# First part in two passes over an x kept on chip, v stored through GpSimd's queue, zeros of the banded weights written after the branch

## The chip, the cores and the metric

The kernel runs on one core of one Trainium2 chip. The metric is the device time of one execution in microseconds (us). All arithmetic is in float32.

## What is computed

The input x has shape 2 x 256 x 64 x 64. Two layers follow one another.

Layer 0 is attention over all 4096 positions of an image, with 8 heads of 32 channels, and a gated mix with the input:

```python
q = proj(Wq, bq) / math.sqrt(hd);  k = proj(Wk, bk);  v = proj(Wv, bv)
attn = softmax(einsum('bnd,bmd->bnm', q, k), axis=-1)
fuse = einsum('bnm,bmd->bnd', attn, v)
hybrid = conv1x1(concatenate([x, fuse], axis=1), Wf, bf)
x = hybrid * m + x * (1.0 - m)          # m: mask, resized to 64 x 64
```

Layer 1 is a channel gate, attention inside windows of 8 x 8 positions with 4 heads, a residual, a channel shuffle, two grouped 7 x 7 convolutions with batch norms, and a sigmoid gate:

```python
x = x * sigmoid(relu(xp @ ca_w1 + ca_b1) @ ca_w2 + ca_b2)
x = x + window_attention(x) @ out_w + out_b
y = relu(bn1(conv7x7(x, sa_w1)))
y = bn2(conv7x7(y, sa_w2))
return x * sigmoid(y)
```

## The kernel before

Positions are cut into 8 chunks of 512 per image, so there are 16 chunks in all. The program has three stretches.

**The first part** runs once over the 16 chunks. It loads a chunk of x (512 KB), multiplies it by Wq, Wk and Wv, and stores q, k and v in DRAM (tensors `qs`, `ks`, `vs`). Each result of two PSUM banks comes from `psum2`, of which there are three buffers. DVE copies q and k with their biases to SBUF (`qst`, `kst`, line 230), ACT squares the same PSUM values (`qsq`, `ksq`, line 231), and both take turns on a bank. TensorE sums the squares per head and token with `headsum` (`nrm`, line 254), and DVE keeps the largest (`nm`, line 265). ACT copies v (`vst`, line 258). The staging tiles have two buffers each, so that a copy waits for the store of two chunks ago. After the last chunk a bound on the scores comes out of `nm`: `top`, a small product `toprow`, `qk2`, `prod` and `flag`. Each engine loads `flag` and branches to one of two arms. Arm "a" uses no shift in the softmax, and it is the one that runs here.

All stores and x loads of the first part are issued by SP, whose DMA queue is q1 in the profile. Weights are loaded through ACT's queue (q10). GpSimd (POOL) issues the set-up of the convolutions through its own queue (q0): mask rows, batch-norm rows, small weights, and the zeros of `ws` (line 389), the DRAM tensor of banded weights, in 16 writes of 896 KB from a tile `zero` in SBUF. The set-up has DVE and ACT steps too (batch norms, products `m1` at line 335 and `m2` at line 374). In this stretch a scheduler of the framework orders each engine's queue.

**The slots** follow after the branch, in an order written out by hand. There are 1024, one for each image, chunk, half of the heads (g) and block of 128 keys (m). In a slot TensorE forms scores for four heads (`sa`, line 580), ACT takes exponentials (`ea`, line 590), TensorE multiplies by v (`ava`, line 609) and DVE adds up denominators (`suma`, line 611). The loop emits the scores of slot i + 2 ahead of the products of slot i. k and v come in pieces of four slots, 256 KB each, from a pool of three buffers: `load_piece` issues k and v of a piece two pieces ahead on SP. Exponentials have 8 buffers. The stage of a finished chunk (the rest of layer 0, and layer 1 up to the convolutions) is spread over later slots. Every sixth slot takes one step of the generator `bands`, which issues a GpSimd DMA that writes one diagonal band into `ws`:

```python
        load_q(0, 0)
        for n in range(AHEAD):
            load_piece(n)
        load_x(0, 0)
        for i in range(2):
            scores(i)()
        for i, (b, c, g, m) in enumerate(slots):
            ...
            if i % 6 == 1:
                next(banded, None)
```

The position of a step in this loop fixes its place in GpSimd's queue. It is no time: GpSimd goes on to its next instruction as soon as that instruction's own waits allow.

**The convolutions** begin among the last 64 slots, read `ws` and the padded rows `xs`, and end the program.

SBUF is reused between the stretches. The tiles of the first part are released ahead of the slots, and the first writers of tiles that lie over them wait for their last readers.

Of the kernel before, what the change touches and what calls it, by code (L numbers as in the profile page):

```python
# [54 lines left out]
def conv_seq_kernel(ctx: ExitStack, tc: tile.TileContext, a, out):  # L55
# [14 lines left out]
    def psum2(name):  # L70
        return ps["pair"].tile([P, 2, CH], F32, tag="s", name=name)

    def psum1(name):
        return ps["one"].tile([P, CH], F32, tag="h", name=name)
# [108 lines left out]

    nm = const.tile([P, B * NCHUNK], F32, name="nm")
    flag = const.tile([1, 1], I32, name="flag")
    with (
        tc.tile_pool(name="w0", bufs=1) as w0,
        tc.tile_pool(name="x0", bufs=3) as x0,
        tc.tile_pool(name="st0", bufs=2) as st0,
    ):  # L190
        def weight(n):
            return load(n, [P, KC, C], a[n].rearrange("(k p) o -> p k o", p=P), nc.scalar, w0)

        wq, wk, wv = weight("WqT"), weight("WkT"), weight("WvT")
        bias = {}
        for n in ("bq", "bk"):
            t = w0.tile([P, KC], F32, name=n)
            for g in range(KC):
                for j in range(HG):
                    h = HG * g + j  # L200
                    nc.scalar.dma_start(
                        t[32 * j : 32 * j + 32, g : g + 1], a[n][h % 2, :, h // 2 : h // 2 + 1]
                    )
            bias[n] = t

        for b in range(B):
            src = a["x"][b].rearrange("(k p) h w -> p k (h w)", p=P)
            for c in range(NCHUNK):
                x = x0.tile([P, KC, CH], F32, tag="x", name=f"x0_{b}_{c}")
                nc.sync.dma_start(x, src[:, :, c * CH : (c + 1) * CH])  # L210
                sqs = []
                for n, w in (("q", wq), ("k", wk)):
                    s = psum2(f"{n}0_{b}_{c}")
                    for g in range(KC):
                        for kc in range(KC):
                            rhs = x[:, kc, :]
                            if n == "q":
                                rhs = rhs.rearrange("p (r w c) -> p w r c", r=WS, w=NW)
                            nc.tensor.matmul(  # L219
                                s[:, g, :],  # L220
                                w[:, kc, g * P : (g + 1) * P],
                                rhs,
                                start=(kc == 0),
                                stop=(kc == KC - 1),
                            )
                    t = st0.tile([P, KC, CH], F32, tag=n, name=f"{n}st_{b}_{c}")
                    sq = st0.tile([P, KC, CH], F32, tag="sq", name=f"{n}sq_{b}_{c}", bufs=4)
                    bt = bias["b" + n]
                    for g in range(KC):
                        nc.vector.tensor_scalar_add(t[:, g, :], s[:, g, :], bt[:, g : g + 1])  # L230
                        nc.scalar.activation(  # L231
                            sq[:, g, :], s[:, g, :], AF.Square, bias=bt[:, g : g + 1]
                        )
                    sqs += [sq[:, g, :] for g in range(KC)]
                    if n == "q":
                        nc.sync.dma_start(q_s[b, c], t.rearrange("p g n -> p (g n)"))
                    else:
                        for g in range(KC):
                            nc.sync.dma_start(k_s[b, g, c], t[:, g, :])
                s = psum2(f"v0_{b}_{c}")  # L240
                sv = s.rearrange("p a (t o) -> p (a t) o", t=2)
                for m in range(4):
                    for kc in range(KC):
                        nc.tensor.matmul(
                            sv[:, m, :],
                            x[:, kc, m * P : (m + 1) * P],
                            wv[:, kc, :],
                            start=(kc == 0),
                            stop=(kc == KC - 1),
                        )  # L250

                norms = psum1(f"nrm_{b}_{c}")
                for i, sq in enumerate(sqs):
                    nc.tensor.matmul(
                        norms[32 * i : 32 * i + 32, :], headsum, sq, start=True, stop=True
                    )
                v = st0.tile([P, KC, 4, P], F32, tag="v", name=f"vst_{b}_{c}")
                nc.scalar.copy(
                    v.rearrange("p g m d -> p m g d"),
                    sv.rearrange("p m (g d) -> p m g d", g=KC),  # L260
                )
                for g in range(KC):
                    nc.sync.dma_start(v_s[b, g, c], v[:, g].rearrange("p m d -> p (m d)"))
                i = b * NCHUNK + c
                nc.vector.tensor_reduce(nm[:, i : i + 1], norms, AX.X, ALU.max)


        top = w0.tile([P, 1], F32, name="top")
        nc.vector.tensor_reduce(top, nm, AX.X, ALU.max)
        row = psum2("toprow")  # L270
        nc.tensor.matmul(row[0:1, 0, 0:P], top, ident, start=True, stop=True)
        qk2 = w0.tile([1, 2], F32, name="qk2")
        nc.vector.tensor_reduce(
            qk2, row[0:1, 0, 0:P].rearrange("p (i r) -> p i r", i=2), AX.X, ALU.max
        )
        prod = w0.tile([1, 1], F32, name="prod")
        nc.vector.tensor_mul(prod, qk2[:, 0:1], qk2[:, 1:2])
        nc.vector.tensor_scalar(flag, prod, (SAFE / SCALE0) ** 2, None, ALU.is_le)

    wf = load("WfT", [P, 2 * KC, C], a["WfT"].rearrange("(k p) o -> p k o", p=P), nc.scalar)  # L280
    bv = load("bv", [P, KC], a["bv"], nc.scalar)
# [103 lines left out]

    zero = cwp.tile([P, 2 * 32 * UW], F32, name="zero")
    nc.gpsimd.memset(zero, 0.0)
    for u in range(NU):
        nc.gpsimd.dma_start(w_s[u], zero)

    r1_s = dram.tile([rows, NU, UW], F32, name="r1s")
    nc.gpsimd.dma_start(
# [22 lines left out]
    def bands():  # L415
        band1 = w_s.rearrange("u p (m f) -> u (p m) f", f=UW)
        band2 = w_s.rearrange("u p (m f) -> u (p m) f", f=UW // 4)
        for q in range(4):
            for dy in range(KS):
                r0, r1 = max(0, dy - PAD), min(RB, RB + dy - PAD)  # L420
                p0, m0, n = 32 * q + 1 + r0, 1 + r0 - dy + PAD, r1 - r0
                k = KS * q + dy
                at0, step = p0 * 64 + m0, 64 + 1
                nc.gpsimd.dma_start(
                    band1[:, at0 : at0 + step * (n - 1) + 1 : step, :], spread(r1_s[k : k + 1], n)
                )
                yield
                for i in range(4):
                    at0, step = p0 * 256 + 128 + i * 32 + m0, 256 + 1
                    nc.gpsimd.dma_start(  # L430
                        band2[:, at0 : at0 + step * (n - 1) + 1 : step, :],
                        spread(r2_s[k : k + 1, :, i], n),
                    )
                    yield
            for i in range(4):
                at0 = 32 * q * 256 + 128 + i * 32 + 1
                nc.gpsimd.dma_start(
                    band2[:, at0 : at0 + RB, :], spread(r2_s[32 + q : 33 + q, :, i], RB)
                )
                yield  # L440
# [30 lines left out]
    def pipeline(arm, shifted, pools):  # L471
# [40 lines left out]
        def load_q(b, c):  # L512
            q = qp.tile([P, KC, CH], F32, tag="q", name=f"q{arm}_{b}_{c}")
            nc.sync.dma_start(q, q_s[b, c].rearrange("p (g n) -> p g n", g=KC))
            qts[b, c] = q
# [572 lines left out]
                stages.popleft()  # L1088

        banded = bands()  # L1090
        load_q(0, 0)
        for n in range(AHEAD):
            load_piece(n)
# [3 lines left out]
        for i, (b, c, g, m) in enumerate(slots):  # L1097
            now[0] = i
            if (b, c, g, m) == (B - 1, NCHUNK - 1, 0, 0):
                conv = convolve()  # L1100
                next(conv)
            if m % PB == 0:
                load_piece(i // PB + AHEAD)
            if g == KC - 1 and m == 0:
                nxt = (b, c + 1) if c + 1 < NCHUNK else (b + 1, 0)
                if nxt[0] < B:
                    load_q(*nxt)
            rest = scores(i + 2) if i + 2 < len(slots) else None
            products(i)
            if rest:  # L1110
                rest()
            if g == KC - 1 and m == NMB - 1:
                at(13, lambda b=b, c=c: stages.append(stage(b, c)))
            run_later()
            if i % 6 == 1:
                next(banded, None)
            if i % 4 == 0:
                run_stages()
# [98 lines left out]
```

## Time and profile before

| | |
|---|---|
| median of 3 runs | 3069.18 us (3069.12 to 3074.34) |
| profiled execution, own time | 3070.01 us |
| its span, first to last instruction | 3068.2 us |
| mean granted TensorE clock | 0.989 |
| first product of the first part begins | 5.29 us |
| first exponential of the slots begins | 222.47 us |
| zero writes of `ws` | 16 of 896 KB, median 17.1 us from issue to landing |
| bytes in the first 220 us | 53.23 MB, 242 GB/s |

In the profile a line gives the engine, the line of the kernel, the operation, the output and inputs by name, their shapes, and how many there are. A product in float32 appears as two records, so four products of q appear as "x8". In the timeline the first two columns are start and duration in us, and brackets at the end give the idle time before and what ended it. "SPq" and "POOLq" are DMAs issued by that engine.

### The profile page before, as it was taken

The numbers are of one execution on the slowest core, as the hardware profiler recorded it, in microseconds if no ns is written. First come the engines' busy times: TensorE is split into PE (matmuls) and PEld (weight loads), VectorE is DVE, ScalarE is ACT, GpSimd is POOL, SyncE is SP. The second block draws the span as 40 slices with busy tenths as digits, with TensorE's granted clock in tenths as the row PEclk, the third lists the DMA queues.
The fourth block names the chain that finished last, engine by engine and source line by source line (L and its number), as shares of the span: only waits on it lengthen the run. The fifth ranks groups of instructions, "written<-read, shape, count | busy, mean of one in ns | idle before, by whom it ended". The sixth has DMA issues, their size and how long they took to land.

```text
span 3068.2 us, 61291 instructions
## 1 busy us (share of the span) xinstructions
PE 2988.2 (97%) x25338; PEld 1015.0 (33%) x25338; DVE 2516.5 (82%) x1398; ACT 2450.6 (80%) x4122; POOL 344.7 (11%) x591
## 2 busy tenths in 40 slices
PE   8989989999999999999999999999999999999897
PEld 4442222232222222222232222323232223224675
DVE  3229989999999999998999999999999998988211
ACT  2239879898989898998989898989898988987423
POOL 7110000001010101010101001010101010000346
PEclk9989999999999999999999999999999999999998
DMA  6953112314141413242322214132413242314264
GB/s 197 356 162 76 59 50 64 67 63 72 59 81 60 75 64 69 66 75 68 66 66 61 66 59 73 59 74 61 78 60 68 70 71 66 109 57 134 61 203 97
DMA packets 160352, 264.20 MB, mean 86 GB/s; under 512 B 43944, under 2 KB 62620, under 8 KB 160064
## 3 DMA queue, kind: packets, MB, share of 16 engines
q1 hardware_dynamic: 133664, 221.72, 24.4%
q0 software_dynamic: 22432, 35.91, 8.4%
q8 instruction: 201, 3.29, 0.4%
q10 hardware_dynamic: 3968, 2.57, 0.3%
q14 instruction: 87, 0.71, 0.1%
HBM read 197.89 MB, written 65.21 MB: 86 GB/s over the span
## 4 chain that ended last, share of the span: by engine, by line
PE 70%; DVE 16%; issue 2%; DMA 2%; ACT 2%; POOL 1%; SPq 0%; DVEq 0%; ACTq 0%; POOLq 0%
PE sa L580 28%; PE ava L609 26%; DVE suma L611 15%; PE qka L748 4%; PE hya L677 4%; PE vwa L834 2%; PE c2a L1011 1%; POOL out_dram L1039 1%; PE c1a L987 1%; ACT ea L590 1%; PE opa L898 1%; DMA out_dram<-za 1%; PE sca L782 1%; PE rda L647 1%; PE pta L857 1%
## 5 line engine op out<-in xcount | busy, mean ns | idle before, releaser
L611 DVE TENSOR_TENSOR suma<-suma,ea 128x2048 f32<-128x2048 f32 x960 | 2198.7, 2290 | 86.0 <-ACT ea L590 1.8
L590 ACT ACTIVATE ea<-sa 128x512 f32<-128x512 f32 (+1 forms) x3072 | 2044.2, 745 | 85.0 <-PE sa L580 36.9
L580 PE MATMUL sa<-qa,ka 32*128 32x512 f32 x8192 | 1189.9, 641 | 8.2 <-DMA ka<-ks 8.0
L609 PE MATMUL ava<-ea,va 128*32 128x512 f32 x8192 | 1092.3, 605 | 0.3 <-ACT fa L619 0.3
L580 PEld LDWEIGHTS sa<-qa,ka 32*128 32x128 f32 x8192 | 333.1, 183 | 762.8 <-ACT ea L590 688.6
L609 PEld LDWEIGHTS ava<-ea,va 128*32 128x32 f32 x8192 | 161.6, 108 | 780.6 <-issue 754.3
L924 POOL DMA_DIRECT2D xs<-xo x94 | 65.9, 708 | 2353.5 <-DVE xo L909 2353.4
L1039 POOL DMA_DIRECT2D out_dram<-za x192 | 108.0, 571 | 128.1 <-DVE za L1033 92.4
L748 PE MATMUL qka<-ua,qkv_w 128*128 128x512 f32 x256 | 118.4, 605 | 0.7 <-DVE ua L738 0.7
L1033 DVE TENSOR_TENSOR za<-za,xla 128x768 f32<-128x768 f32 (+1 forms) x16 | 20.9, 1309 | 101.4 <-ACT za L1027 65.0
L1011 PE MATMUL c2a<-yca,wa 32*128 32x192 f32 (+1 forms) x1400 | 100.0, 427 | 0.3 <-ACT za L1021 0.3
L685 ACT ACTIVATE ta<-hya,bf 128x512 f32<-128x512 f32 x32 | 20.2, 684 | 96.9 <-PE hya L677 96.9
L1011 PEld LDWEIGHTS c2a<-yca,wa 32*128 32x128 f32 x1400 | 91.8, 316 | 10.9 <-issue 9.7
L689 DVE TENSOR_TENSOR ta<-ta,mca 128x512 f32<-128x512 f32 x32 | 22.0, 689 | 88.0 <-ACT ta L685 88.0
L1021 ACT ACTIVATE za<-c2a 128x384 f32<-128x384 f32 (+1 forms) x50 | 26.3, 578 | 79.7 <-DMA out_dram<-za 47.9
L803 ACT ACTIVATE ewa<-ewa,mxwa 128x64 f32<-128x64 f32 x256 | 85.5, 362 | 0.0
L611 DVE TENSOR_TENSOR suma<-ea,ea 128x2048 f32<-128x2048 f32 x32 | 73.1, 2286 | 15.0 <-DMA va<-vs 15.0
L231 ACT ACTIVATE qsq<-q,bq 128x512 f32<-128x512 f32 x32 | 22.0, 687 | 74.1 <-DVE qst L230 72.6
L430 POOL DMA_DIRECT2D ws<-r2s x112 | 69.5, 623 | 68.5 <-DMA xs<-xo 33.2
L761 ACT ACTIVATE qka<-qka,qkv_b 128x512 f32<-128x512 f32 x64 | 40.7, 694 | 44.2 <-PE qka L748 44.2
L987 PE MATMUL c1a<-xla,wa 128*32 128x192 f32 (+1 forms) x896 | 58.7, 413 | 14.2 <-DMA xla<-xs 14.2
L230 DVE TENSOR_SCALAR qst<-q,bq 128x512 f32<-128x512 f32 x32 | 24.0, 751 | 59.1 <-PE q L219 41.2
(139 smaller groups left out, 1674.7 us busy)
## 6 DMA issues: line engine op xcount, KB each, us to landing
ka<-ks SPq DMA_DIRECT2D x256, 256.0 KB
va<-vs SPq DMA_DIRECT2D x256, 256.0 KB
ws<-zero POOLq DMA_DIRECT2D x16, 896.0 KB, 17.1
wa<-ws SPq DMA_DIRECT2D x16, 896.0 KB
xs<-xo POOLq DMA_DIRECT2D x78, 140.0 KB, 7.2
xla<-xs SPq DMA_DIRECT2D x23, 420.0 KB
x<-in_x_dram SPq DMA_DIRECT2D x16, 512.0 KB
ks<-kst SPq DMA_DIRECT2D x32, 256.0 KB
```

The costliest lines, as they stand in the source:

```text
L430: nc.gpsimd.dma_start(band2[:, at0 : at0 + step * (n - 1) + 1 : step, :], spread(r2_s[k : k + 1, :, i], n),)
L580: nc.tensor.matmul(heads[j], k[r, cols], q[r, g, :], start=True, stop=not shifted)
L590: nc.scalar.activation(e[:, h, :], tile, AF.Exp, scale=SCALE0)
L609: nc.tensor.matmul(av[r, :], v[:, m % PB, r], e[:, j, :], start=start, stop=stop)
L611: nc.vector.tensor_add(total, first[0] if m == 1 else total, e)
L677: nc.tensor.matmul(s[:, oc, :], wf[:, kc, oc * P : (oc + 1) * P], xw[kc] if kc < KC else f[:, kc - KC, :], start=(kc == 0), stop=(kc == 2 ...
L748: nc.tensor.matmul(s[:, j, :], wqkv[:, kc, o : o + P], u[:, kc, :], start=(kc == 0), stop=(kc == KC - 1),)
L803: nc.scalar.activation(e[:, n, :], e[:, n, :], AF.Exp, bias=mx[:, n : n + 1], accum_out=rs[:, n : n + 1],)
L924: eng.dma_start(x_s[b, n, p + r0 : p + r1].rearrange("r g w -> g r w"), xo[64 * h : 64 * h + 64, oc, r0 - WS * c : r1 - WS * c, :],)
L987: nc.tensor.matmul(s[32 * j : 32 * j + 32, 0 : n * W], w[:, j, d, :], xs[k][:, 0:n, j, d : d + W], start=(d == 0), stop=(d == KS - 1),)
L1011: nc.tensor.matmul(tiles[j // 2][:, j % 2, 0 : n * W], w[r, d], y[r, 0:n, d : d + W], start=(d == 0), stop=(d == KS - 1),)
L1039: eng.dma_start(dst[b, i, r0:r1, UG * u : UG * u + UG, :], z[p + r0 : p + r1, :, nb * m + n, :],)
```

## The change

- The loop over chunks becomes two. Pass 1 loads x, forms q and k, and stores them. All 16 chunks of x stay in SBUF: the pool `x0` has one buffer per chunk, and is opened after the staging pool. Pass 2 forms v from them.
- The squares of q and k of a chunk go to one tile. DVE takes the largest of each four neighbouring tokens (`tops`, one instruction for 2048 elements), and `headsum` multiplies these 128 columns instead of 512 (function `norms`). It does so one chunk late, after the next chunk's q. The last chunk's norm and `flag` are computed during the first two chunks of pass 2.
- Stores of v are issued by GpSimd instead of SP.
- The 16 zero writes are replaced by one write of 896 KB to a DRAM tensor `zeros` in the first part, and four copies from there into `ws`, each for four of its 16 slices, as the first steps of `bands`. The source's first dimension has step zero. The rest of `bands` comes four steps later, and is drained ahead of the convolutions.
- One exponential of a single element (`warm`) stands ahead of the slots on ACT.

In the queues as built, GpSimd's four copies stand directly after its branch and ahead of all bands, each as 4 x 14 x 16384 floats, without a wait for another engine. The stores of v stand behind GpSimd's set-up. SP's order after the branch is q, k and v of pieces 0 and 1, x, mask, k and v of piece 2, as before. The first exponential and the load of x wait for the last stores of v.

```diff
-        tc.tile_pool(name="x0", bufs=3) as x0,
         tc.tile_pool(name="st0", bufs=2) as st0,
+        tc.tile_pool(name="x0", bufs=1) as x0,
...
+        def norms(i, tops):
+            s = psum1(f"nrm_{i}")
+            for n in range(2 * KC):
+                s_ = s[32 * n : 32 * n + 32, 0 : CH // 4]
+                nc.tensor.matmul(s_, headsum, tops[:, n, :], start=True, stop=True)
+            nc.vector.tensor_reduce(nm[:, i : i + 1], s[:, 0 : CH // 4], AX.X, ALU.max)
+
+        xs0, last = [], None
+        for i, (b, c) in enumerate(chunks):
+            x = x0.tile([P, KC, CH], F32, name=f"x0_{b}_{c}")
...
+                if n == "q":
+                    nc.sync.dma_start(q_s[b, c], t.rearrange("p g n -> p (g n)"))
+                    if i:
+                        norms(i - 1, last)
...
+            nc.vector.tensor_reduce(
+                tops, sq.rearrange("p g (n f) -> p g n f", f=4), AX.X, ALU.max
+            )
+            last = tops
...
+        for i, (b, c) in enumerate(chunks):
+            x = xs0[i]
+            s = psum2(f"v0_{b}_{c}")
...
             for g in range(KC):
-                nc.sync.dma_start(v_s[b, g, c], v[:, g].rearrange("p m d -> p (m d)"))
+                nc.gpsimd.dma_start(v_s[b, g, c], v[:, g].rearrange("p m d -> p (m d)"))
+            if i == 0:
+                norms(len(chunks) - 1, last)
+                nc.vector.tensor_reduce(top, nm, AX.X, ALU.max)
+            elif i == 1:
...
-    for u in range(NU):
-        nc.gpsimd.dma_start(w_s[u], zero)
+    zero_s = dram.tile([P, 2 * 32 * UW], F32, name="zeros")
+    nc.gpsimd.dma_start(zero_s, zero)
...
     def bands():
+        for u in range(0, NU, 4):
+            nc.gpsimd.dma_start(
+                w_s[u : u + 4].rearrange("u p f -> u (p f)"),
+                zero_s.rearrange("p f -> (p f)").unsqueeze(0).to_broadcast([4, P * 64 * UW]),
+            )
+            yield
...
         banded = bands()
+        nc.scalar.activation(warm, ones[0:1, 0:1], AF.Exp)
...
             if (b, c, g, m) == (B - 1, NCHUNK - 1, 0, 0):
+                for _ in banded:
+                    pass
```

More of the change, by code (lines that the diff above doesn't have):

```diff
@@ L185, in conv_seq_kernel @@
     flag = const.tile([1, 1], I32, name="flag")
+    warm = const.tile([1, 1], F32, name="warm")
     with (
         tc.tile_pool(name="w0", bufs=1) as w0,
-        tc.tile_pool(name="x0", bufs=3) as x0,
         tc.tile_pool(name="st0", bufs=2) as st0,
+        tc.tile_pool(name="x0", bufs=1) as x0,
     ):
@@ L204, in conv_seq_kernel @@
             bias[n] = t
-        for b in range(B):
-            src = a["x"][b].rearrange("(k p) h w -> p k (h w)", p=P)
[L208 to L242, printed above, removed]
@@ new lines, in conv_seq_kernel @@
+        chunks = [(b, c) for b in range(B) for c in range(NCHUNK)]
+        def norms(i, tops):
[7 more added lines that the diff above has]
+            x = x0.tile([P, KC, CH], F32, name=f"x0_{b}_{c}")
+            src = a["x"][b].rearrange("(k p) h w -> p k (h w)", p=P)
+            nc.sync.dma_start(x, src[:, :, c * CH : (c + 1) * CH])
+            xs0.append(x)
+            sq = st0.tile([P, 2 * KC, CH], F32, tag="sq", name=f"sq_{b}_{c}")
+            tops = st0.tile([P, 2 * KC, CH // 4], F32, tag="top4", name=f"top4_{b}_{c}")
+            for n, w in (("q", wq), ("k", wk)):
+                s = psum2(f"{n}0_{b}_{c}")
+                for g in range(KC):
@@ L243, in conv_seq_kernel @@
                     for kc in range(KC):
+                        rhs = x[:, kc, :]
+                        if n == "q":
+                            rhs = rhs.rearrange("p (r w c) -> p w r c", r=WS, w=NW)
                         nc.tensor.matmul(
-                            sv[:, m, :],
-                            x[:, kc, m * P : (m + 1) * P],
-                            wv[:, kc, :],
+                            s[:, g, :],
+                            w[:, kc, g * P : (g + 1) * P],
+                            rhs,
@@ L250, in conv_seq_kernel @@
                         )
[L252 to L255, printed above, removed]
-                    )
[L257 to L260, printed above, removed]
-                )
@@ L262, in conv_seq_kernel @@
-                for g in range(KC):
-                    nc.sync.dma_start(v_s[b, g, c], v[:, g].rearrange("p m d -> p (m d)"))
[L264 to L278, printed above, removed]
+                t = st0.tile([P, KC, CH], F32, tag=n, name=f"{n}st_{b}_{c}")
+                bt = bias["b" + n]
+                for g in range(KC):
+                    nc.vector.tensor_scalar_add(t[:, g, :], s[:, g, :], bt[:, g : g + 1])
+                    nc.scalar.activation(
+                        sq[:, g + KC * (n == "k"), :], s[:, g, :], AF.Square, bias=bt[:, g : g + 1]
+                    )
@@ new lines, in conv_seq_kernel @@
+                if n == "q":
+                    nc.sync.dma_start(q_s[b, c], t.rearrange("p g n -> p (g n)"))
+                    if i:
+                        norms(i - 1, last)
+                else:
+                    for g in range(KC):
+                        nc.sync.dma_start(k_s[b, g, c], t[:, g, :])
+            nc.vector.tensor_reduce(
+                tops, sq.rearrange("p g (n f) -> p g n f", f=4), AX.X, ALU.max
+            )
+            last = tops
+        row = psum2("toprow")
@@ new lines, in conv_seq_kernel @@
+        top = w0.tile([P, 1], F32, name="top")
+        for i, (b, c) in enumerate(chunks):
+            x = xs0[i]
+            s = psum2(f"v0_{b}_{c}")
+            sv = s.rearrange("p a (t o) -> p (a t) o", t=2)
+            for m in range(4):
+                for kc in range(KC):
+                    nc.tensor.matmul(
+                        sv[:, m, :],
+                        x[:, kc, m * P : (m + 1) * P],
+                        wv[:, kc, :],
+                        start=(kc == 0),
+                        stop=(kc == KC - 1),
+                    )
+            v = st0.tile([P, KC, 4, P], F32, tag="v", name=f"vst_{b}_{c}")
+            nc.scalar.copy(
+                v.rearrange("p g m d -> p m g d"),
+                sv.rearrange("p m (g d) -> p m g d", g=KC),
+            )
+            for g in range(KC):
+                nc.gpsimd.dma_start(v_s[b, g, c], v[:, g].rearrange("p m d -> p (m d)"))
[3 more added lines that the diff above has]
+            elif i == 1:
+                nc.tensor.matmul(row[0:1, 0, 0:P], top, ident, start=True, stop=True)
+                qk2 = w0.tile([1, 2], F32, name="qk2")
+                nc.vector.tensor_reduce(
+                    qk2, row[0:1, 0, 0:P].rearrange("p (i r) -> p i r", i=2), AX.X, ALU.max
+                )
+                prod = w0.tile([1, 1], F32, name="prod")
+                nc.vector.tensor_mul(prod, qk2[:, 0:1], qk2[:, 1:2])
+                nc.vector.tensor_scalar(flag, prod, (SAFE / SCALE0) ** 2, None, ALU.is_le)
@@ L417, in bands @@
         band2 = w_s.rearrange("u p (m f) -> u (p m) f", f=UW // 4)
+        for u in range(0, NU, 4):
+            nc.gpsimd.dma_start(
+                w_s[u : u + 4].rearrange("u p f -> u (p f)"),
+                zero_s.rearrange("p f -> (p f)").unsqueeze(0).to_broadcast([4, P * 64 * UW]),
+            )
+            yield
         for q in range(4):
```

## The prediction

> **What bounds the kernel now.** I read the page's busy shares, its chain that ended last, and then the timeline up to the first exponential, which is where the change lies.
>
> ```profile
> PE 2988.2 (97%) x25338; PEld 1015.0 (33%) x25338; DVE 2516.5 (82%) x1398; ACT 2450.6 (80%) x4122; POOL 344.7 (11%) x591
> ...
> PE 70%; DVE 16%; issue 2%; DMA 2%; ACT 2%; POOL 1%; SPq 0%; DVEq 0%; ACTq 0%; POOLq 0%
> ```
>
> TensorE sets the time nearly everywhere, so a microsecond of TensorE work or of TensorE waiting is a microsecond of the span. In the first part, one steady chunk on TensorE and the end of that part read (start, duration, what, idle time before):
>
> ```profile
> 162.52 3.70 PE L219 MATMUL q<-x,WqT 128*128 128x512 f32 x8
> 166.06 3.60 PE L219 MATMUL k<-x,WkT 128*128 128x512 f32 x8
> 169.49 3.62 PE L244 MATMUL v<-WvT,x 128*128 128x256 f32 x16
> 173.04 0.62 PE L254 MATMUL nrm<-qsq,headsum 128*32 128x512 f32 x2
> ...
> 174.04 3.70 PE L219 MATMUL q<-x,WqT 128*128 128x512 f32 x8
> ...
> 210.05 1.05 PE L452 MATMUL bvf<-bv,WfT 128*128 128x1 f32 x8
> 219.07 3.79 PE L580 MATMUL sa<-qa,ka 32*128 32x512 f32 x14 [7.96 <-DMA ka<-ks]
> ```
>
> A chunk takes 11.51 us: q 3.54, k 3.43, v 3.55, norms 0.99. Sixteen would be 184.2; from 5.29 to 208.6 they take 203.3. The other 19.1 are waits: about 3 at the start, 8.4 in chunks 3 and 4 (DVE and ACT wait there for small weight loads on GpSimd's queue), 7.4 in chunks 8 and 9 (stores stuck beside the zero writes). After the last product:
>
> ```profile
> 211.39 0.14 DVE L278 TENSOR_SCALAR flag<-prod 1x1 int32<-1x1 f32 x1
> 212.59 0.32 SPq L514 DMA_DIRECT2D qa<-qs  x1
> ...
> 221.18 1.28 ACT L590 ACT_TABLE_LOAD   x1 [12.43 <-PE sa L580]
> 222.47 3.90 ACT L590 ACTIVATE ea<-sa 128x512 f32<-128x512 f32 x6
> ```
>
> Flag, branch, first k load and table load lie one after another: 13.9 us from 208.6 to the first exponential at 222.47.
>
> **What the Trainium skill says.** "DMA: Bandwidth & Descriptors", section Queues, rings and completion order: each DMA engine round-robins between its queues by whole packets, whatever their size. The trace agrees. While the zeros were written (100 to 110 us; packets, MB, share):
>
> ```profile
> q0 software_dynamic: 502, 3.20, 76.6%
> q1 hardware_dynamic: 506, 0.96, 24.9%
> ```
>
> One packet each, although q0's are 7 KB and q1's 2 to 4 KB. The same page, Rules for kernel authors: an outermost zero-step dimension of c copies confines a DMA to at most c engines; nothing in this trace shows it. Its Latency and other measured facts: a DRAM-to-DRAM copy ran at some 207 to 214 GB/s; the trace has no large one, but its plateau of 417 GB/s, each byte touching DRAM once, halves to 208. "ScalarE: Activation LUTs", What ACT_TABLE_LOAD costs, has 1283 ns; the trace has 1.28 us.
>
> **Part by part: the first part.** Pass 1 keeps q (3.54), k (3.43) and norms. Norms multiply 128 columns instead of 512: a quarter of 0.99 plus switching, 0.5 taken (0.25 to 0.8). So 7.4 us a chunk on TensorE. DVE gets one maximum over 2048 elements per chunk; the nearest row has 512 in 0.68:
>
> ```profile
> L794 DVE TENSOR_REDUCE mxwa<-ewa 128x8 f32<-128x512 f32 x32 | 21.8, 682 | 42.5 <-ACT ewa L790 42.5
> ```
>
> An add of 2048 takes 2.29 (L611), so 2.3 (4 if groups of four cost extra). The norm's maximum falls from 0.69 to about 0.28 (L273's row, 128 elements). DVE then has 4 x 0.75 + 2.3 + 0.28 = 5.6 per chunk. Its dependent loop (maximum, copy, norm maximum, copy, copy, square, copy, square) is 2.3 + 0.75 + 0.28 + 0.75 + 0.75 + 0.8 + 0.75 + 0.75 = 7.1: just under TensorE. Walking the built queues with these rows: copies of chunk 4 stand behind the m1 product, whose loads end at about 51.5 (50.96 before; GpSimd starts its mask stores 1.2 later), some 7 us of waiting; those of chunk 6 behind the m2 products until about 73. From there TensorE paces; pass 1 ends at about 135.6.
>
> Pass 2 is 16 x 3.45 = 55.2, with the last norm and the small top product 0.7: last v product at **191.5**. Its stores move to GpSimd's queue: 32 issues of about 0.55, behind set-up that ends near 95, so none is late. Each copy (1.0) waits for the stores of two chunks ago: 6.9 us minus copy and two issues leaves 4.6 for landing; I take 2.5 to 3.5, so it is hidden. Sixteen x loads move ahead on SP; one is needed each 7.4 us, hidden. Branch and first loads now go beneath pass 2, as the flag is ready near 149. What is late next: the first exponential's buffer lies over the v staging, and its wait includes the last v stores: 0.2 + 1.0 + 1.2 + 2.5, so about 197. `warm` takes its 1.28 inside that wait. **Gain 222.5 - 197 = 25.5 us** (18 to 30).
>
> **The zeros.** Leaving the first part they take away the 7.4 of chunks 8 and 9, counted above. One 896 KB write remains there, hidden. Among the slots, nothing makes GpSimd wait between the four copies: a slot is only a place in its queue, so all four issue (4 x 0.55) right after its branch, data from about 196. Each is built as 4 x 14 x 16384 floats, first source step zero: 4 engines, 14 packets of 64 KB on each; four DMAs fill 16 engines once. 14.7 MB at 208 to 214 GB/s: **70 us** (37 if engines keep the 26 GB/s each that 417/16 gives).
>
> Who waits: SP's q1. Its order after the branch is q, k0, v0, k1, v1, then x, mask, k2, v2. The x load waits for the last v stores (its tile lies over them), so x, mask, k2 and v2 join q1 as the zeros start: 16 + 8 + 8 + 8 packets of 2 KB per engine. At one q1 packet per 64 KB packet only 14 pass in 70 us. Pieces need this pace:
>
> ```profile
> 229.76 0.32 SPq L507 DMA_DIRECT2D ka<-ks  x1
> 234.83 0.32 SPq L509 DMA_DIRECT2D va<-vs  x1
> 238.02 0.32 SPq L507 DMA_DIRECT2D ka<-ks  x1
> 243.15 0.32 SPq L509 DMA_DIRECT2D va<-vs  x1
> ```
>
> A pair every 8.3 us, 16 packets per engine: a neighbour packet above about 0.5 us starves it. At 70/14 it is 5 us. Slots 0 to 7 run on pieces 0 and 1. Scores of slot 8 are due 16.4 us after the first exponential (228.5 + 5 x 2.07 against 222.47), at 213.5; k2 lands at 196 + 70 + 2.5 = 268.5. TensorE waits 55 us and restarts at a low clock (0.70 in 222 to 232 before): 2 more. The bands queue behind the zeros on GpSimd, but the weights are only loaded at 2655.8 before; free. Afterwards k and v are ahead again.
>
> **Sum.** 3068.2 - 25.5 + 57 = 3099.7; with the 1.8 around the span 3101.5, against 3070.0 for the profiled execution; the median shown is 0.8 lower: **3101**.
>
> **Rivals.** (1) *No starvation, faster*: descriptors of 64 KB are chopped, or engines share by bytes. With 4 KB packets q1 would get a third of some 300 GB/s, above the 62 it needs (512 KB per 8.3 us). Then 3069 - 25.5 = 3044. Against it: the equal counts above, and 16 KB instruction packets on the page (q8: 201 packets, 3.29 MB) left whole. It decides below 0.5 us a packet. (2) *Fast copies*: 37 us, k2 at 235.5, wait 22 + 2: 3068. (3) *All four DMAs on the same four engines*: 56 packets there, 141 us at 26 GB/s; v3 at about 340 instead of slot 12's 227, some 112 lost: 3156. (4) *The maximum costs 4 us*: the loop is 8.8, 16 x 1.4 = 22 more on any case; little speaks for it.
>
> **How the numbers follow.** This kernel's measurement tells 0.2% (6 us) from no change. Chances: starvation at 70 us 0.47, all on four engines 0.13, fast copies 0.12, none 0.24, slow maximum 0.04. Slower: 0.47 + 0.13 + 0.02 + 0.04 = 0.66; same 0.07 (most of the rest of fast copies); faster 0.27. The likeliest case's own range is 3080 to 3120 (50 to 85 us of copying). To hold 8 in 10 the range reaches down to rival 1 and leaves out rival 3: 3040 to 3130.
>
> **What would show it.** Right: v products end near 191, first exponential near 197; then a TensorE gap of some 50 us before slot 8's scores, ended by DMA ka<-ks, with equal packet counts of q0 and q1 and few of both. Wrong: slots at 2.07 us through the zeros, or k2 landing within 20 us of issue; pass 1 above 8 us a chunk with DVE never idle; v copies that wait for v stores.

## Result and the profile after

The changed kernel takes 3091.68 us (median of 4 runs, 3087.66 to 3095.37) against 3069.57 us for the kernel before: a ratio of 1.0065, with a 95% interval of 1.005 to 1.008. The change makes the kernel 0.65% slower. The profiled execution took 3095.37 us with a span of 3093.6 us (before: 3068.2).

From the page of the changed kernel come the busy shares, the chain that ended last, and the group of the scores (busy time, mean ns of one, then the idle time before it and its releasers):

```profile
PE 2973.6 (96%) x25338; PEld 1013.4 (33%) x25338; DVE 2544.0 (82%) x1414; ACT 2450.1 (79%) x4123; POOL 356.3 (12%) x612
...
PE 83%; DVE 7%; DMA 4%; ACT 2%; POOL 2%; another core or an unknown queue 1%; issue 1%; SPq 0%; DVEq 0%; ACTq 0%; POOLq 0%
...
L602 PE MATMUL sa<-qa,ka 32*128 32x512 f32 x8192 | 1187.6, 641 | 38.9 <-DMA ka<-ks 35.8
```

TensorE is busy for 14.6 us less than before, yet the span is 25.4 us longer, so the time is in waits. The last line names the wait: the scores stand idle for 35.8 us until a load of k has landed.

The timelines of the changed kernel show the new DVE maximum, and one steady chunk of pass 1 on TensorE:

```profile
22.91 2.27 DVE L254 TENSOR_REDUCE top<-sq 128x512 f32<-128x2048 f32 x1
...
102.84 3.60 PE L233 MATMUL q<-x,WqT 128*128 128x512 f32 x8
106.28 2.74 PE L233 MATMUL k<-x,WkT 128*128 128x512 f32 x6
108.94 0.43 PE L215 MATMUL nrm<-top,headsum 128*32 128x128 f32 x8
109.30 1.13 PE L233 MATMUL k<-x,WkT 128*128 128x512 f32 x2
110.26 3.17 PE L233 MATMUL q<-x,WqT 128*128 128x512 f32 x7
```

From one q to the next is 7.42 us. The norms stand inside it, between the products of k, and TensorE has no pause. So far the change does what it says. Then the slots begin, in the timeline of all engines:

```profile
199.41 2.73 POOL L435 DMA_DIRECT2D ws<-zeros  x4 [0.53 <-issue]
201.36 5.80 ACT L612 ACTIVATE ea<-sa 128x512 f32<-128x512 f32 x9 [2.33 <-issue]
...
203.32 1.56 SPq L529 DMA_DIRECT2D ka<-ks  x1
...
215.85 1.14 PE L602 MATMUL sa<-qa,ka 32*128 32x512 f32 x8
...
253.83 2.09 PE L602 MATMUL sa<-qa,ka 32*128 32x512 f32 x8 [35.85 <-DMA ka<-ks]
253.96 0.65 POOL L446 DMA_DIRECT2D ws<-r1s  x1 [51.83 <-DMA ws<-zeros]
```

The four zero copies leave back to back at 199.41, and the first exponential begins at 201.36, 21.1 us earlier than before. The k of piece 2 is issued 4 us after the copies and is due at about 218. It lands at 253.8, in the same moment as the last bytes of the copies. The DMA view from 210 to 230 us shows how the time went (packets, MB, share of the 16 engines):

```profile
q0 software_dynamic: 96, 6.29, 93.6%
q1 hardware_dynamic: 96, 0.20, 4.8%
```

The queues pass equal numbers of packets, 96 to 96, but a zero packet is 64 KB and a q1 packet 2 KB. A turn of both takes a DMA engine 3.3 us (20 us x 16 engines / 96), nearly all of it for the zero packet, and q1 gets 10 GB/s of 325. From 220 to 250 us TensorE does nothing and its granted clock is 0.50 to 0.56; the first scores after the wait take 2.09 us instead of 1.14.

**Where the 25.4 us of the profiled execution lie:**

| place | us |
|---|---|
| first exponential at 201.36, not 222.47 | -21.1 |
| wait ahead of slot 8 | +35.9 |
| restart at a low clock (first slots after it 3.88 and 2.56 us apart, not 2.07) | +2.3 |
| won back around chunk 0's stage, 340 to 420 us; not traced | -2.8 |
| one pause of 3.5 us at 2040 and the slow products after it, in this execution | +4.7 |
| drift over the other slots | -0.2 |
| last exponential to GpSimd's last store | +1.8 |
| GpSimd's last store to the end | +4.8 |

Such a pause ("issue" in the waits, 2 to 4 us) shows in several of the runs below too; its cause is open. It may be part of why this execution is the slowest of the four; the other three have no trace.

### The profile page after: what moved, and what is told of

It is laid out like the page before. It is cut to its first block, busy times and chain, and to the rows that moved or that the text cites. A ratio compares the mean times of both kernels' runs of the same rounds, so it can differ in the third digit from the quotient of the medians.

```text
span 3093.6 us, 61287 instructions
## 1 busy us (share of the span) xinstructions
PE 2973.6 (96%) x25338; PEld 1013.4 (33%) x25338; DVE 2544.0 (82%) x1414; ACT 2450.1 (79%) x4123; POOL 356.3 (12%) x612
## 4 chain that ended last, share of the span: by engine, by line
PE 83%; DVE 7%; DMA 4%; ACT 2%; POOL 2%; another core or an unknown queue 1%; issue 1%; SPq 0%; DVEq 0%; ACTq 0%; POOLq 0%
PE sa L602 33%; PE ava L631 30%; DVE suma L633 6%; PE qka L770 4%; PE hya L699 4%; PE vwa L856 2%; PE v L268 2%; PE opa L920 2%; DMA wa<-ws 1%; PE c2a L1033 1%; POOL out_dram L1061 1%; PE k L233 1%; PE q L233 1%; PE c1a L1009 1%
## 5 line engine op out<-in xcount | busy, mean ns | idle before, releaser
L602 PE MATMUL sa<-qa,ka 32*128 32x512 f32 x8192 | 1187.6, 641 | 38.9 <-DMA ka<-ks 35.8
L244 ACT ACTIVATE sq<-q,bq 128x512 f32<-128x512 f32 x32 | 22.0, 687 | 65.2 <-DVE qst L243 58.0
L770 PEld LDWEIGHTS qka<-ua,qkv_w 128*128 128x128 f32 x256 | 46.0, 189 | 72.4 <-issue 58.8
```

Of the source, the lines that this page charges most:

```text
L602: nc.tensor.matmul(heads[j], k[r, cols], q[r, g, :], start=True, stop=not shifted)
L770: nc.tensor.matmul(s[:, j, :], wqkv[:, kc, o : o + P], u[:, kc, :], start=(kc == 0), stop=(kc == KC - 1),)
```

## Experiments

The theory, called **turns** below: the stall is set by the packets of q1 that stand ahead of piece 2, and by how long one packet of the zeros takes. Its first rival, **bytes**: the copies take the DMA bandwidth, and whatever their packets are, the loads wait until they are through. Other rivals put the loss into the two passes, the load of x, or GpSimd's new stores. In the experiments the kernel before ran at 3073 to 3075 us, 4 to 5 us above the result's, so ratios are compared. The times expected for the runs up to xlate start from the result's 3091.7 and would lie some 4 us higher on the scale of these runs. All times in the two right columns, and starts of the first exponential, are those of the profiled executions.

| kernel | median us | ratio to before, 95% interval | wait for loads in the first slots, us | GpSimd's last store to the end, us |
|---|---|---|---|---|
| changed kernel | 3091.7 | 1.0065 (1.005 to 1.008) | 35.9 | 11.3 |
| z28 | 3095.0 | 1.0070 (1.0053 to 1.0087) | 34.0 | 10.8 |
| z14 | 3075.8 | 1.0012 (1.0002 to 1.0023) | 19.4 + 2.1 | 11.0 |
| z7 | 3063.6 | 0.9965 (0.9952 to 0.9978) | 6.2 | 11.8 |
| zfirst | 3057.7 | 0.9960 (0.9946 to 0.9974) | 0 | 11.3 |
| full | 3062.6 | 0.9968 (0.9958 to 0.9978) | 0 | 11.6 |
| bz64 | 3095.5 | 1.0073 (1.0056 to 1.009) | 22.3 + 8.4 | 5.2 |
| vsp | 3094.3 | 1.0065 (1.0048 to 1.0082) | 36.6 in pass 2 | 5.4 |
| xlate | 3080.3 | 1.0022 (1.0014 to 1.003) | 26.9 | 11.2 |
| vact | 3058.6 | 0.9949 (0.9934 to 0.9963) | 0 | 6.7 |
| z7x | 3056.1 | 0.9945 (0.9931 to 0.996) | 0 | 11.9 |
| best | 3055.2 | 0.9936 (0.9915 to 0.9957) | 0 | 6.8 |

The last column of the kernel before is 6.5 us.

### z28, z14, z7: the same bytes in smaller packets

```diff
             nc.gpsimd.dma_start(
-                w_s[u : u + 4].rearrange("u p f -> u (p f)"),
-                zero_s.rearrange("p f -> (p f)").unsqueeze(0).to_broadcast([4, P * 64 * UW]),
+                w_s[u : u + 4].rearrange("u p f -> u (p f)").rearrange("u (n f) -> n u f", n=128),
+                zero_s.rearrange("p f -> (p f)")
+                .rearrange("(n f) -> n f", n=128)
+                .unsqueeze(1)
+                .to_broadcast([128, 4, P * 64 * UW // 128]),
             )
```

128 pieces give packets of 7 KB (z7); 64 give 14 KB (z14), 32 give 28 KB (z28).

> The changed kernel with its zero copies in packets of 28 KB instead of 64 KB; same bytes, same place. Turns (each DMA engine passes one packet of the zeros for one packet of q1): the changed kernel's trace shows 3.3 us per 64 KB packet, 19.7 GB/s per engine, so 1.4 us per 28 KB packet; k2 is the 32nd q1 packet of an engine after the x load is issued at 201.4, 32 x 1.5 = 48 us, past the end of the copies at about 246, so k2 lands as late as before, or a few us earlier: wait of TensorE ahead of slot 8 some 33 us, time 3088. Bytes (the loads wait because the copies take the bandwidth, whatever the packets are): 36 us, 3091.

> The changed kernel with its zero copies in packets of 14 KB. Turns: 0.7 us per packet of the zeros plus 0.1 for q1's own, k2 passes after 32 x 0.8 = 26 us, about 228; with some 2.5 us to land, TensorE waits about 15 to 20 us ahead of slot 8 (due 218), and v2 follows 6 us later: time about 3072 to 3076. Bytes: a wait of 36 us again, 3091.

> The changed kernel with its zero copies in packets of 7 KB, the size that the kernel before used for its zero writes. Turns: 0.36 us per packet of the zeros plus 0.1, k2 passes after 32 x 0.46 = 15 us at 216, v2 after 18 us: no wait ahead of slot 8, or up to 3 us; time 3091.7 - 36 = 3055 to 3058, faster than before. Bytes: 36 us, 3091.

The waits ahead of slot 8 were 34.0, 19.4 and 6.2 us for 28, 14 and 7 KB, against 35.9 for 64 KB (z14 waits another 2.1 us ahead of slot 12). From the TensorE timelines of z28, z14 and z7:

```profile
252.76 2.09 PE L605 MATMUL sa<-qa,ka 32*128 32x512 f32 x8 [34.02 <-DMA ka<-ks]
```

```profile
237.05 2.09 PE L605 MATMUL sa<-qa,ka 32*128 32x512 f32 x8 [19.39 <-DMA ka<-ks]
```

```profile
225.87 2.09 PE L605 MATMUL sa<-qa,ka 32*128 32x512 f32 x8 [6.17 <-DMA ka<-ks]
```

The same DMA view, 210 to 230 us, first z28, then z14, then z7:

```profile
q0 software_dynamic: 251, 6.28, 88.4%
q1 hardware_dynamic: 251, 0.48, 10.9%
```

```profile
q0 software_dynamic: 437, 5.82, 79.8%
q1 hardware_dynamic: 436, 0.82, 18.1%
```

```profile
q0 software_dynamic: 775, 5.38, 76.3%
q1 hardware_dynamic: 771, 1.43, 23.9%
```

The counts stay one to one, and q0 loses little (6.29 to 5.38 MB in 20 us), but q1 gets 2.6, 4.5 and 8 times as many packets. Bytes expected 36 us in all three; it falls. For 28 KB the k of piece 2 again lands with the last bytes of the copies (252.8), so almost nothing is gained, as turns expected. The edit also changes the order of the copies (the outermost dimension is 32, 64 or 128 instead of 4). z28 has the new order with packets that are still large, and waits nearly as long: the order is not what helps.

Two times missed. z28 took 3095.0, not 3088: about 4 us are the scale of these runs, and its profiled execution has three pauses of the kind named above (4.8 us). z7 took 3063.6, not 3055 to 3058, where turns expected at most 3 us of wait and got 6.2. The count was low: from 203 to 226 us q1 passed 691 packets, 43 per engine, and in z14 685 until its scores started, again 43, where I had counted 32. So packets of later loads go by before the last of piece 2's k has landed. Whether they overtake it on one engine, or some engines run ahead of the slowest, the trace does not show. The pace of 0.53 us in z7 (23 us / 43) was also above the 0.46 assumed.

### zfirst: the zeros back in the first part

```diff
-    zero_s = dram.tile([P, 2 * 32 * UW], F32, name="zeros")
-    nc.gpsimd.dma_start(zero_s, zero)
+    for u in range(NU):
+        nc.gpsimd.dma_start(w_s[u], zero)
...
     def bands():
-        for u in range(0, NU, 4):
-            nc.gpsimd.dma_start(...)
-            yield
```

> The changed kernel with the zeros written as in the kernel before: 16 writes of 896 KB from SBUF in the first part, none among the slots. If the stall ahead of slot 8 is all the work of the copies it is gone: the first part's gain of 21 us stays unless the zero writes hold up its stores as they did before (7.4 us in chunks 8 and 9 there; v stores behind them on GpSimd's queue have until pass 2), so 3049 to 3057. If the stall comes from the load of x or from the first part in two passes (loads of k and v reading what was stored late), it stays: 3085 or more.

```profile
205.15 5.79 ACT L606 ACTIVATE ea<-sa 128x512 f32<-128x512 f32 x9 [2.31 <-issue]
```

No wait for k is left after that, and the time is 0.4% below the kernel before. So the two passes, the early branch and the rest of the change are a gain, and the zeros are the loss. The price of writing them in the first part is smaller: the copies of k wait for their stores (6.7 us on DVE in all), and the first exponential comes at 205.15 instead of 201.36.

### full: without the maximum of four

```diff
-                s_ = s[32 * n : 32 * n + 32, 0 : CH // 4]
+                s_ = s[32 * n : 32 * n + 32, :]
...
-            nc.vector.tensor_reduce(
-                tops, sq.rearrange("p g (n f) -> p g n f", f=4), AX.X, ALU.max
-            )
-            last = tops
+            last = sq
```

The rest is zfirst.

> The changed kernel with the zeros written in the first part (as in zfirst), and the squares summed for all 512 tokens again: no maximum of four on DVE, norms of 512 columns on TensorE. TensorE paces (my theory of the first part): norms go from 0.43 back to about 1.0, 16 x 0.56 = 9 us more than zfirst, less what TensorE waited there for the maximum (about 10 us in five chunks, 4 of them in one where DVE waited for a small load and waits again): 3058 to 3066. DVE paces (its loop with the maximum was the limit in more chunks than the waits name): without 2.3 us per chunk on DVE the first part gets shorter, 3050 or less.

In its timeline the norms of a chunk take 1.06 us, and the chunk 8.06 (from 131.20 to 139.26):

```profile
109.80 1.06 PE L215 MATMUL nrm<-sq,headsum 128*32 128x512 f32 x8
```

The first exponential comes at 209.35, 4.2 us later than in zfirst. The medians differ by 4.9 us, but the ratios by 0.0008 alone, some 2.5 us and within their intervals. TensorE paces pass 1, and the maximum is a small gain: 4.2 us in these two traces, not told apart in the times. It is below 16 x 0.63 = 10 us because the maximum brings waits of its own: in zfirst TensorE stands 10.1 us for it in five chunks, while full waits some 5 us for squares instead.

### bz64: the zeros part alone, in the kernel before

```diff
-    for u in range(NU):
-        nc.gpsimd.dma_start(w_s[u], zero)
+    zero_s = dram.tile([P, 2 * 32 * UW], F32, name="zeros")
+    nc.gpsimd.dma_start(zero_s, zero)
...
     def bands():
+        for u in range(0, NU, 4):
+            nc.gpsimd.dma_start(
+                w_s[u : u + 4].rearrange("u p f -> u (p f)"),
+                zero_s.rearrange("p f -> (p f)").unsqueeze(0).to_broadcast([4, P * 64 * UW]),
+            )
+            yield
```

> The kernel before with the zeros part of the change alone: one 896 KB write to DRAM in the first part, four copies in 64 KB packets after the branch. Turns: here q, k and v of pieces 0 and 1 are issued after the branch too, at the same time as the copies, so they also pass one packet for 64 KB; some 14 packets of an engine pass in the 46 us of copying, and piece 1's k is the 17th or later. Nearly the whole copying shows: 7 us gained in chunks 8 and 9 of the first part, then 35 to 45 us lost, time 3097 to 3108. If the changed kernel's stall needs the two passes (x load and pieces late for another reason), the time is 3062.

The loss needs none of the rest: ratio 1.0073. Its timeline has two waits among the first slots, the first for a v of the pieces that are issued with the copies:

```profile
241.97 1.93 PE L615 MATMUL ava<-ea,va 128*32 128x512 f32 x8 [22.32 <-DMA va<-vs]
255.58 2.09 PE L586 MATMUL sa<-qa,ka 32*128 32x512 f32 x8 [8.44 <-DMA ka<-ks]
```

Together they are 30.8 us, less than the 35 to 45 expected, and the first exponential comes 6.7 us earlier (215.74 against 222.47), as the zeros no longer disturb the first part: 24.1 us lost, where the span is 23.3 us longer. The time, 3095.5, is below the 3097 to 3108 expected.

### vsp: the stores of v by SP

```diff
-                nc.gpsimd.dma_start(v_s[b, g, c], v[:, g].rearrange("p m d -> p (m d)"))
+                nc.sync.dma_start(v_s[b, g, c], v[:, g].rearrange("p m d -> p (m d)"))
```

> The changed kernel with the stores of v issued by SP again, not by GpSimd. Turns: the stores end before the copies begin, so the wait ahead of slot 8 stays at 36 us and the time at 3091, if SP's 32 issues do not come late. GpSimd rival (the stores on its queue delay the last v, the first exponential, or the end of the program by lengthening GpSimd's instruction stream): first exponential earlier than 201.4, or the 11.3 us between GpSimd's last store and the end of the span back at 6.5 as in the kernel before; 3080 to 3087.

The time came as turns expected, but not where: with no store of v in its queue GpSimd reaches its branch when the flag is ready, and the copies run beside pass 2. There the stores of v on SP's queue wait their turn behind 64 KB packets. From its timeline of all engines:

```profile
149.51 2.57 POOL L435 DMA_DIRECT2D ws<-zeros  x4 [64.32 <-issue]
...
200.60 1.01 ACT L276 COPY vst<-v 128x1024 f32<-128x1024 f32 x1 [44.79 <-DMA vs<-vst]
...
201.67 4.63 PE L268 MATMUL v<-WvT,x 128*128 128x256 f32 x10 [36.59 <-ACT vst L276]
```

So the stall follows the copies to whatever shares the DMA engines with them. My assumption that the stores of v would end before the copies begin was wrong: the store move is what holds the copies back until pass 2 is over. The other half of the expectation, the rival's, was right too: the end of the program is back at 5.4 us.

### xlate: x and mask after piece 2

```diff
-        load_x(0, 0)
         for i in range(2):
             scores(i)()
...
             if m % PB == 0:
                 load_piece(i // PB + AHEAD)
+            if i == 0:
+                load_x(0, 0)
```

> The changed kernel with x and mask of the first chunk loaded after k and v of piece 2 instead of ahead of them; nothing else. SP no longer stops at the x load's wait, so k and v of piece 2 are issued near 152, 50 us ahead of the copies. Turns: no wait ahead of slot 8; piece 3 (issued at about 209) is now the 16 + 8 + 8 = 32nd q1 packet of an engine and lands after the copies as piece 2 did, at about 252, but is due 8.3 us later than piece 2 (slot 12, 226): wait 26 to 28 us, time 3082 to 3084. Bytes or a fixed cost of the copies on TensorE: 36 us wherever it falls, 3091.

SP now issues the k of piece 2 at 150.94 and its v at 158.10, and the wait moves to slot 12 and shrinks to what turns gave it, 26 to 28 us, as the timeline of TensorE shows:

```profile
251.71 2.09 PE L602 MATMUL sa<-qa,ka 32*128 32x512 f32 x8 [26.88 <-DMA ka<-ks]
```

The time, 3080.3, is below the 3082 to 3084 expected; the wait does not account for that, and the rest is open.

### vact, z7x and best: the end of the program, and a version that beats both

vact is zfirst with the stores of v issued by ACT; z7x is z7 with xlate's order; best is z7x with

```diff
+            eng = nc.gpsimd if i == len(chunks) - 1 else nc.scalar
             for g in range(KC):
-                nc.gpsimd.dma_start(v_s[b, g, c], v[:, g].rearrange("p m d -> p (m d)"))
+                eng.dma_start(v_s[b, g, c], v[:, g].rearrange("p m d -> p (m d)"))
```

> The changed kernel with the zeros written in the first part (as in zfirst) and the stores of v issued by ACT, neither by GpSimd nor by SP. No zeros among the slots: no stall. End of the program: in the runs so far the time from GpSimd's last store to the end is 11.1 to 11.8 us where GpSimd issues v's 32 stores and 5.2 to 6.5 where it does not, and one 8 KB instruction packet more is fetched. If it is the length of GpSimd's instruction stream, the end falls back to 5 to 6.5, and the time is zfirst's 3057.7 less 5: 3051 to 3054, faster than both kernels. If the end belongs to the two passes or to x on chip, it stays at 11: 3057.

> The changed kernel with two things altered: zero copies in packets of 7 KB (as in z7), and the first x and mask loaded after piece 2 (as in xlate). Turns: piece 3 is the 32nd q1 packet of an engine behind the x load, about 15 us at 0.46 us, so near 218 to 220, and is due at 226: no wait ahead of slot 8 (6.2 us in z7) nor of slot 12. Time z7's 3063.6 less 6: 3056 to 3059. If a fixed part of the wait remains whatever the order, 3063.

> z7x with the stores of v issued by ACT, but those of the last chunk by GpSimd: GpSimd's stream is 30 instructions shorter, and its zero copies still stand behind the last store of v. If the length of GpSimd's stream sets the end, 5 to 6.5 us from its last store to the end instead of 11.9, 87 instruction packets of 8 KB instead of 88, and the time 3050 to 3053. ACT's rival: 30 DMA issues on ACT lengthen pass 2 or delay the first exponential (207.6 in vact, where also the bands ran beside pass 2) and eat the gain: 3055 to 3059. In both, no wait for ka beyond the first slots.

The last stores of the program, from the timelines of GpSimd, in the kernel before (span 3068.2), the changed kernel (3093.6) and best (3054.3):

```profile
3048.23 13.45 POOL L1039 DMA_DIRECT2D out_dram<-za  x24 [2.87 <-DVE za L1033]
```

```profile
3068.82 13.47 POOL L1061 DMA_DIRECT2D out_dram<-za  x24 [2.88 <-DVE za L1055]
```

```profile
3034.03 13.47 POOL L1065 DMA_DIRECT2D out_dram<-za  x24 [2.89 <-DVE za L1059]
```

Start plus duration, taken from the span, leaves 6.5, 11.3 and 6.8 us. Every kernel in which GpSimd issues all 32 stores of v has 10.8 to 11.9, every other one 5.2 to 6.8, with one and with two passes. The pages differ in one row beside it: queue q14 carries 88 instruction packets in the first kind and 87 in the second. Here the changed kernel, then best:

```profile
q14 instruction: 88, 0.72, 0.1%
```

```profile
q14 instruction: 87, 0.71, 0.1%
```

These counts go with the end in all thirteen kernels, the kernel before included. How the one leads to the other is open: in the changed kernel the last q14 packet runs alone at 3083.9, after all data, but in best one does so too, at 3049.2, and the span goes on for some 9 us after the first and 5 us after the second. Shown is that 30 or 32 fewer stores on GpSimd take 4.6 to 5.9 us off the end.

z7x has no wait for k or v left and came as expected, 3056.1. vact and best got their shorter ends, but hardly in the times. vact took 3058.6, not 3051 to 3054, and best 3055.2, which is in the range that the rival for ACT gave. Their ratios lie 0.0011 and 0.0009 below those of zfirst and z7x, within the intervals. In their profiled executions the first exponential came 2.5 us later than in zfirst and 2.6 later than in z7x (its releaser is the last stores of v). Best beats the kernel before by 0.64% and the changed kernel by 1.3% (0.9936 / 1.0065); z7x and best can't be told apart.

## Why the prediction was right

It said slower, with 3101 us, and slower it was: 3091.7. By its own steps:

- **Pass 1 on TensorE, the maximum, the norms**: right. A chunk takes 7.42 us (7.4), the maximum 2.27 (2.3), the norms 0.43 (0.5).
- **Waits in the first part**: mis-sized. The start cost more: the copies of the first chunk's k waited for the loads of its bias until 20.43, and the first three chunks took 29.2 us instead of 22.3 (3 x 7.42), where 3 us had been allowed. The 7 us that were given to m1 came at that place (5.8 in the chunk from 34.79, 1.2 in the next), but with DVE standing for the small load `ca_b`. The m2 products held up a maximum, for which TensorE waited 1.5 us at 79.26. Pass 1 ended at 139.94, not 135.6.
- **Pass 2 and the first exponential**: 16 chunks of 3.45 and hidden v stores, as said; everything 4.4 us late from pass 1. The first exponential began at 201.36, not 197: a gain of 21.1 instead of 25.5, inside the range given (18 to 30).
- **The zero copies' place and shape**: right. They issue at 199.41 in one go, 64 KB packets fill the engines (93.6% of 16), and q1 gets one packet for each, as the Trainium skill's page "DMA: Bandwidth & Descriptors", Queues, rings and completion order, has it.
- **The rate of the copies**: the term that was most mis-sized. I took 207 to 214 GB/s from the Trainium skill, "DMA: Bandwidth & Descriptors", Latency and other measured facts, and 208 from halving the plateau of 417. That row is of copies of 128 x 16 KiB tiles whose rows lie 512 KiB or more apart, issued by SP or ACT. The copies here are contiguous, come from GpSimd, and read the same 896 KB sixteen times; which of these counts, no run here shows. The trace has 6.29 MB in 20 us, 314 GB/s. Nearly all large packets were through after some 47 us, the last four ended as late as 253.0, 52 us after the first, and k landed at 253.8, not 268.5. The measurement decides: bytes that are read and written in DRAM did not cost double here (417 / 314 = 1.3).
- **The stall**: 35.9 us, not 55. k landed 14.7 us earlier, by the copies' rate, and was due 4.4 us later. The restart cost 2.3 us, as said (2).
- **The weights**: free, as said; GpSimd's 51.8 us behind the zeros hurt nothing.
- **Not seen**: 4.8 us at the end, from a longer GpSimd stream. That the stores on GpSimd also hold the copies back was taken from the built queues, but its weight was not: vsp showed it.

From 3101.5 for the profiled execution: -19.1 (stall), +4.4 (gain), +0.3 (restart), +6.6 (end), -2.8 and +4.5 (table above) give 3095.4, the time measured. The direction and the mechanism were right, but that the number came so close is luck: errors of both signs nearly cancelled. With the stall and the restart as measured and all else as forecast the sum would have been 3082.7.

Of the rivals, "no starvation" is excluded by the equal counts. "Fast copies" (37 us of copying, 22 of stall) lay nearer than the likeliest case (70 and 55): measured were 47 to 52 and 35.9. Its sum, 3068, is yet farther from the time. "All on the same four engines" would show 12 idle engines; the share was 93.6% of 16. "The maximum costs 4 us" fell at 2.27.

## What to carry to other kernels

A DMA engine that alternates between queues packet by packet makes every queue pay for the largest packet of its neighbour: before moving a big copy beside small loads, multiply the packets ahead of the critical load by the time of one neighbour packet (here 3.3 us for 64 KB). The load is late by that product or until the big copy is through, whichever comes first. Cut the neighbour's packets until it fits. A place in a queue without a wait is no time: ask which wait ahead of it really holds it, for here it was the stores of v. Put loads whose buffers come free late behind those that are due first.

## What was unexpected about the hardware

- A DRAM-to-DRAM copy in 64 KB packets, with a source that repeats, ran at 314 GB/s beside a trickle of loads, 19.7 GB/s per DMA engine.
- Large packets gained little for the copy itself: with 7 KB it still moved 269 GB/s (5.38 MB in 20 us), while q1 moved 72 GB/s instead of 10.
- Some 30 more DMA instructions early in GpSimd's stream cost 4.6 to 5.9 us at the end of the program, nearly 3000 us later. The cause is open.
